# Four small moves in a convolution, scan and attention kernel: products three states ahead, gated sums sooner, x loaded first, the shortest output last

## The chip, the cores and the metric

The kernel runs on one core of a Trainium2 chip. A core has five engines that run side by side, each with a queue of its own: TensorE (PE, matrix products; PEld is its loading of weights), VectorE (DVE), ScalarE (ACT), GpSimd (POOL) and SyncE (SP, which here only issues DMAs). They meet through semaphores. Times are microseconds (us) of device time for one execution. The profile is one more execution, recorded by the hardware.

## What is computed

Input x has 8 images of 128 channels with 16 x 16 pixels, all float32. Four layers follow each other:

- an "adder" convolution: for each of 128 filters f, minus the sum over channels and 3 x 3 taps of |W - x|, on normalised images;
- a Mamba block with three scan directions, two images (512 columns) at a time:

```
uc    = silu(causal_conv1d(u))
delta = softplus(dt @ dw.T + db)
h_t   = exp(delta_t * A) * h_(t-1) + (delta_t * u_t) * B_t      # 16 states per channel
y     = sum over states of h * C + u * D
```

  and then an attention between the directions, a gate with silu(z) and two 3 x 3 convolutions;
- an attention layer with random features, and a mixture of experts;
- a spectral layer, whose result is the output.

## The kernel before

**Adder layer** (`adder_layer`, `start`). Eight images lie beside each other, 128 channels on the partitions. x is loaded as four pairs of images: pairs 0 and 2 are issued on SP's queue, pairs 1 and 3 on ACT's. Behind them on SP stand the weights w of this layer and of the next ones, and behind them on ACT three shared tables (`cst`, `vecs`, `rows`). `start` normalises the images pair by pair: a sum on DVE (L333), a mean through a product on PE (`mu`), squares on ACT (`sq`), their sums, a variance through a product (`var`), and the scaled images `sh` in three shifted copies. Between these small products PE is given spare ones (`meanwhile`), whose results nobody reads. Then PE sums the taps of x into `px`, in six taps of four blocks of two images, and the columns of w into `wsum`; in the first tap `wsum` products stand between the blocks. After that, for each filter and tap, DVE (a maximum, L450 and L446) or ACT (an absolute value, L452) makes `d`, 2048 columns, and PE sums it over the channels into `o`. `d` has four buffers for each of the two engines.

**Scans** (`_scans`). Twelve units (four pairs of images, three directions) of 16 states each make 192 states r, with n the state within its unit. For each state:

- POOL multiplies `du` (delta times u) by a row of B into `dbu` (`inputs`, L814), three buffers;
- ACT makes the decays `da` (`decays`, L827), in PSUM, three buffers;
- DVE runs two scans (L909), one for each half of the channels, and multiplies the result `st` by a row of C that ACT copied to PSUM (`pcs`, L819; L920). For n = 1 and n = 8 (`AWAY`) POOL makes that product instead (L918);
- PE adds the states up in `acc`.

The rows of B and C come back from DRAM, spread over all partitions, in chunks of two states (`bs` and `cs`, L803), two buffers each, issued on SP. While a unit is scanned, `prepare` makes the inputs of the next one step by step: on POOL these are `uc` (L688), for each half of the channels two steps of `delta` (L668, L669), and `du` (L699). Beside that `other` runs the attention and convolutions of the pair before: `images` advances two attention chains a turn at a time, and from a certain turn on the gated sums of `gated` (L1059, L1061, L1063) on POOL; `gates` puts L604 on POOL. The loop below sets the order on PE, DVE, ACT and POOL; what SP issues is ordered by the framework's scheduler, except where the program pins it. The first unit (`first_unit`) is written out by itself; it has spare products of its own.

**Spectral layer** (`spectral_layer`). Five groups of columns are accumulated in PSUM over all filters; at the end each group gets its last three taps, an addition with the residual X on DVE (L1876) and a DMA to the output (L1882). The groups go from the one with the fewest columns (256) to the largest (512).

Of the kernel before, what the change touches and what calls it, by code (L numbers as in the profile page):

```python
# [10 lines left out]
F32 = mybir.dt.float32  # L11
# [5 lines left out]
P = 128  # L17
B = 8
# [3 lines left out]
NBLK = NT // BLK  # L22
# [3 lines left out]
NST = 16  # L26
# [197 lines left out]
class Env:  # L224
# [30 lines left out]
        self.diag = early.tile([P, 3, 2, 5, P], F32, tag="diag", name="diag")  # L255

    def load_shared(self):
        nc = self.nc
        nc.scalar.dma_start(self.cst[:, P:], self.dram["cst"][:, P:])
        nc.scalar.dma_start(self.vecs, self.dram["vecs"])  # L260
        nc.scalar.dma_start(self.rows, self.dram["rows"].partition_broadcast(P))

    def load_weights(self):
        for k, t in self.w.items():
            self.nc.sync.dma_start(t, self.dram[k])
        self.nc.sync.dma_start(self.diag, self.dram["diag"])

    def c(self, name):
        a, b = self.cols["cst"][name]
# [37 lines left out]
MAX_TAPS = (0, 2, 4, 6, 8)  # L307
# [7 lines left out]
def start(E, pool, psum, x, shifted):  # L315

    nc = E.nc
    spare = psum.tile([P, P], F32, tag="px", name="spare")

    def meanwhile(n):  # L320

        for _ in range(n):
            E.mm(spare, E.ones, E.ones)

    def small(name):
        return pool.tile([P, B], F32, tag=name, name=name)

    s1, neg_mu, s2, rs = (small(n) for n in ("s1", "neg_mu", "s2", "rs"))
    sq = pool.tile([P, B, L], F32, tag="sq", name="sq0")
    pairs = [slice(2 * i, 2 * i + 2) for i in range(NBLK)]  # L330
    meanwhile(6)
    for b in pairs:
        nc.vector.tensor_reduce(s1[:, b], x[:, b, :], AX.X, ALU.add)  # L333
        mu = psum.tile([P, 2], F32, tag="st", name="mu0")
        E.mm(mu, E.c("group"), s1[:, b])
        meanwhile(2 if b is not pairs[-1] else 1)
        nc.scalar.copy(neg_mu[:, b], mu)
        for i in range(b.start, b.stop):
            nc.scalar.activation(sq[:, i, :], x[:, i, :], AF.Square, bias=neg_mu[:, i : i + 1])
    for b in pairs:  # L340
        nc.vector.tensor_reduce(s2[:, b], sq[:, b, :], AX.X, ALU.add)
        var = psum.tile([P, 2], F32, tag="st", name="var0")
        E.mm(var, E.c("group"), s2[:, b])
        meanwhile(1 if b is not pairs[-1] else 2)
        nc.scalar.activation(rs[:, b], var, AF.Sqrt, bias=E.eps, scale=-1.0)
    for b in pairs:
        nc.vector.reciprocal(rs[:, b], rs[:, b])
        for i in range(b.start, b.stop):
            dst = shifted[1][:, i, 1:17, :].rearrange("p h w -> p (h w)")
            nc.vector.tensor_scalar(dst, x[:, i, :], neg_mu[:, i : i + 1], rs[:, i : i + 1], ALU.add, ALU.mult)  # L350
        nc.scalar.copy(shifted[0][:, b, 1:17, 1:16], shifted[1][:, b, 1:17, 0:15])
    for i, b in enumerate(pairs):
        op = nc.vector.tensor_copy if i < 2 else nc.scalar.copy
        op(shifted[2][:, b, 1:17, 0:15], shifted[1][:, b, 1:17, 1:16])


def adder_layer(E):
# [8 lines left out]
    with ExitStack() as ctx:  # L366
# [10 lines left out]
        for i in range(NBLK):  # L377
            two = slice(2 * i, 2 * i + 2)
            (nc.scalar if i % 2 else nc.sync).dma_start(x[:, two, :], E.dram["x"][two].rearrange("b c s -> c b s"))
        w = p.tile([P, 9, P], F32, tag="w", name="w0")  # L380
        nc.sync.dma_start(w, E.dram["adder"])
        E.load_shared()
        E.load_weights()

# [22 lines left out]
            kh, kw = divmod(k, 3)  # L407
            return shifted[kw].rearrange("p b h w -> p b (h w)")[:, :, kh * 16 : kh * 16 + L]

        def add(out, lhsT, src, start, stop, blocks=range(NBLK)):  # L410

            for i in blocks:
                E.mm(out[i * FG : (i + 1) * FG, :], lhsT, src[:, 2 * i : 2 * i + 2, :], start, stop)

        px = ps.tile([P, BLK], F32, tag="px", name="px0")
# [1 line left out]
        with tc.manual_schedule(engines={nc.tensor.engine, nc.vector.engine, nc.scalar.engine}):  # L417
            nc.scalar.preload_act_table_set(SQRT)
            start(E, p, ps, x, shifted)

            wsum = [ps.tile([P, 1], F32, tag="st", name="wsum") for _ in range(2)]
            weights = [(pw, taps, k) for pw, taps in zip(wsum, (MAX_TAPS, MORE_TAPS)) for k in taps]
            for n, k in enumerate(PX_TAPS):
                for i in range(NBLK):
                    add(px, neg[:, int(k in MORE_TAPS), :], tap(k), n == 0, n == len(PX_TAPS) - 1, (i,))
                    for pw, taps, t in weights[2 * i : 2 * i + 2] if n == 0 else ():
                        E.mm(pw, w[:, t, :], E.ones[:, 0:1], start=t == taps[0], stop=t == taps[-1])

# [104 lines left out]
def _scans(E, ctx, F):  # L535
# [165 lines left out]
    def first_unit(k, s, p, new, pre, sig, proj):  # L701
# [66 lines left out]
        for h, (tag, scratch) in enumerate((("f", "ln_xc"), ("cs", "ln_rstd"))):  # L768
            pd = ps.tile([P, UT], F32, tag=tag, name="pd")
            E.mm(pd, w_dt[:, k, h * P : (h + 1) * P], proj[0:DTR, :])  # L770
            one_e = one.tile([P, UT], F32, tag=scratch, name="one_e")
            halves.append((pd, delta[:, h, :], pre[:, h, :], sig[:, h, :], one_e))

        for h, (pd, d, e, r, one_e) in enumerate(halves):
            db = E.v("db" + s, h)
# [34 lines left out]

    def inputs(r):
        if r < states:
            dbs[r] = three.tile([P, 2, UT], F32, tag="db", name="dbu")
            nc.gpsimd.tensor_tensor(dbs[r], got[r // NST]["du"], bc(row("bs", r), 1, 2), ALU.mult)  # L814

    def rows_of_c(r):
# [50 lines left out]
    with tc.manual_schedule(engines={nc.tensor.engine, nc.vector.engine, nc.scalar.engine, nc.gpsimd.engine}):  # L867
        new, *rest = tiles()
        got[0].update(new)
        first = first_unit(*units[0], new, *rest)  # L870
        next(first)
        for c in range(2):
            chunk("bs", 0, c)
            chunk("cs", NST, c)
        dbs[0] = three.tile([P, 2, UT], F32, tag="db", name="dbu")
        for h in range(2):
            next(first)
            nc.vector.tensor_mul(dbs[0][:, h, :], new["du"][:, h, :], row("bs", 0))
            decays(h)
            if h == 0:  # L880
                rows_of_c(0)
        inputs(1)
        next(first)
        decays(2)
    acc = late = None
    room = 0
    other = _Chain(beside())

# [3 lines left out]
    with tc.manual_schedule(engines={nc.tensor.engine, nc.vector.engine, nc.scalar.engine, nc.gpsimd.engine}):  # L892
        for r in range(states):
            i, n = divmod(r, NST)
            k, s, p = units[i]
            if r % (len(BRANCHES) * NST) == 0:
                F.y[p] = F.two.tile([P, 3, 2, UT], F32, tag="y", name="y")
            if n == NST - 2:
                while not more.done:
                    more.advance()  # L900
                more = _Chain(prepare(*units[i + 2], got[i + 2]) if i + 2 < len(units) else iter(()))
            if r % CN == 0:
                chunk("bs", 0, r // CN + 2)
            inputs(r + 2)
            st = four.tile([P, 2, UT], F32, tag="st", name="st")
            for h in range(2):
                g = 2 * r + h
                da = das[g % 3].rearrange("p b l -> p (b l)")
                nc.vector.tensor_tensor_scan(st[:, h, :], da, dbs[r][:, h, :], 0.0, ALU.mult, ALU.add)  # L909
                decays(g + 3)  # L910
            if n == 0:
                if i:
                    result(i - 1, acc)
                acc = ps.tile([P, 2, UT], F32, tag="acc", name="acc")
                for h in range(2):
                    E.mm(acc[:, h, :], E.diag[:, k, h, 4, :], got[i]["uc"][:, h, :], start=True, stop=False)
            if n in AWAY:
                nc.gpsimd.tensor_tensor(st, st, bc(row("cs", r), 1, 2), ALU.mult)  # L918
            else:
                nc.vector.tensor_tensor(st, st, bc(pcs[r][:, :], 1, 2), ALU.mult)  # L920
            rows_of_c(r + 1)
            if r % CN == 0:
                chunk("cs", NST, r // CN + 2)

            ready, late = ([], st) if n in AWAY else ([t for t in (st, late) if t is not None], None)
            for t in ready:
                for h in range(2):
                    E.mm(acc[:, h, :], ident, t[:, h, :], start=False, stop=n == NST - 1)
            room = min(room, 0) + SHARE - more.advance() - (2 if n == 0 else 0)
            if room > 0:  # L930
                room -= other.advance(room)
# [7 lines left out]
class _Fuse:  # L939
# [33 lines left out]
    def images(self, p):  # L973
# [6 lines left out]
        while not (a.done and b.done):  # L980

            a.advance()
            yield b.advance()
            if 4 <= n < 10:
                gate.advance()
            n += 1
            yield LATER
# [813 lines left out]
def spectral_layer(E, W, out):  # L1801
# [8 lines left out]
    with ExitStack() as ctx:  # L1810
# [57 lines left out]
        nc.sync.dma_start(mu, E.dram["Mu"].rearrange("i d t e -> d i t e"))  # L1868
        W.running(E, [mu[:, i].rearrange("p t e -> p (t e)") for i in range(4)])
        X = E.X.rearrange("p (b l) -> p b l", l=L)  # L1870
        for j, (i, lo, hi, b0, b1) in enumerate(groups):
            for k in range(TAPS):
                tap = u[:, b0:b1, TAPS - 1 - k + lo : TAPS - 1 - k + hi]
                E.mm(acc[j], mu[:, i, k, :], tap.rearrange("p b (i q) -> p b q i", q=2), start=False, stop=k == TAPS - 1)
# [45 lines left out]
```

## Time and profile before

| | |
|---|---|
| Runs, median (lowest to highest) | 2990.8 us (2988.36 to 2991.7, 3 runs) |
| The profiled execution's own time | 2994.82 us |
| Its span in the profile | 2993.0 us |
| PE busy | 2857.9 us (95%) |
| DVE busy | 2421.7 us (81%) |
| ACT busy | 2268.3 us (76%) |
| POOL busy | 700.4 us (23%) |
| Start to the first `o` product | 0 to about 30 us |
| Adder | to 953 us |
| Scans | 984 to about 1700 us |
| Attention layers, experts | to about 2760 us |
| Spectral layer | to 2993 us |

A row of the profile names line, engine, operation, `output<-inputs` by the program's tile names, shapes and a count; then busy time and mean, and after the second bar how long the engine stood idle just before such instructions and who ended most of that. In the timeline a row has start, length and, in brackets, the idle time before it. In the chain, each row is a stretch of the work that ended last. Busy shares are averages over stages; within a stage the wait that ends last counts. All but 24 of the 192 states cost DVE at least 3.57 us.

### The profile page before, as it was taken

The page shows a single profiled execution, that of the slowest core. Times are in us where ns is not written, and L with a number is a line of the kernel's source. Part 1 is how long each engine was busy: PE and PEld are TensorE (multiplying, and loading weights), DVE is VectorE, ACT ScalarE, POOL GpSimd, SP SyncE. Part 2 cuts the span into 40 slices and gives each one's busy share as a digit, 9 for nine tenths or more (in the row PEclk, how much of TensorE's full clock was granted, in tenths as well). Part 3 has the DMA queues.
Part 4 walks back from the last instruction along what each step waited for, and adds up shares of the span by engine and source line. Part 5 has one row for each costly group of instructions (what it writes and reads, how often), then busy time and mean ns, then how long its engine had stood idle before and what let it go on. Part 6 is the DMA issues. An engine that isn't in the chain of part 4 may idle for free.

```text
span 2993.0 us, 41823 instructions
## 1 busy us (share of the span) xinstructions
PE 2857.9 (95%) x16404; PEld 1281.7 (43%) x16404; DVE 2421.7 (81%) x3398; ACT 2268.3 (76%) x2740; POOL 700.4 (23%) x415
## 2 busy tenths in 40 slices
PE   9999999999999788998898998999999999999999
PEld 4222222222223233443343454556555555664444
DVE  7999999999998899999899747887787787885210
ACT  7999999999997777777777434477878887778332
POOL 0000000000000799998999500000000000000100
PEclk9999999999999999999999999999999999999999
DMA  1000000000000534444343200000000000001100
GB/s 68 1 1 5 1 1 5 1 1 5 1 1 5 174 145 146 135 148 144 125 163 135 101 4 25 14 1 14 14 1 14 14 12 3 14 1 45 51 28 14
DMA packets 39482, 133.46 MB, mean 45 GB/s; under 512 B 7522, under 2 KB 10732, under 8 KB 37748
## 3 DMA queue, kind: packets, MB, share of 16 engines
q1 hardware_dynamic: 38164, 129.46, 12.5%
q8 instruction: 129, 2.11, 0.3%
q10 hardware_dynamic: 1120, 1.32, 0.1%
q14 instruction: 69, 0.57, 0.1%
HBM read 127.88 MB, written 1.84 MB: 43 GB/s over the span
## 4 chain that ended last, share of the span: by engine, by line
PE 68%; DVE 15%; ACT 9%; POOL 4%; issue 3%; DMA 1%; DVEq 0%; ACTq 0%; POOLq 0%
PE o L289 29%; PE p L289 8%; DVE st L909 5%; PE acc L289 5%; PE g L289 4%; PE conv L289 3%; PE pc L289 2%; PE var L289 2%; PE pf L289 2%; POOL dbu L814 2%; PE pa L289 1%; ACT L1173 1%; PE pq L289 1%; ACT da L827 1%; PE pconv L289 1%
## 5 line engine op out<-in xcount | busy, mean ns | idle before, releaser
L289 PE MATMUL o<-d,sel 128*32 128x512 f32 x8512 | 921.5, 593 | 2.0 <-DVE d L446 1.2
L452 ACT ACTIVATE d<-sh,w 128x2048 f32<-128x2048 f32 x472 | 900.2, 1995 | 28.6 <-PE o L289 28.5
L450 DVE TENSOR_SCALAR d<-sh,w 128x2048 f32<-128x2048 f32 x592 | 718.4, 1281 | 15.0 <-PE o L289 14.9
L814 POOL TENSOR_TENSOR dbu<-du,bs 128x1024 f32<-128x1024 f32 x191 | 446.6, 2365 | 980.2 <-DVE du L786 974.7
L289 PEld LDWEIGHTS o<-d,sel 128*32 128x32 f32 x8512 | 278.3, 110 | 644.5 <-issue 533.5
L909 DVE TENSOR_TENSOR_SCAN st<-da,dbu 128x512 f32<-128x512 f32 x384 | 446.3, 1207 | 18.1 <-POOL dbu L814 14.2
L289 PE MATMUL acc<-st,cst 128*128 128x512 f32 x768 | 375.2, 621 | 52.9 <-DVE st L920 52.6
L827 ACT ACTIVATE da<-delta,neg_a 128x510 f32<-128x510 f32 x384 | 257.6, 687 | 78.6 <-DVE st L909 73.2
L289 PEld LDWEIGHTS acc<-st,cst 128*128 128x128 f32 x768 | 144.5, 196 | 252.6 <-issue 143.8
L920 DVE TENSOR_TENSOR st<-st,pcs 128x1024 f32<-128x1024 f32 x168 | 205.2, 1222 | 18.8 <-ACT pcs L819 1.5
L446 DVE SCALAR_TENSOR_TENSOR d<-sh,w,d 128x2048 f32<-128x2048 f32 x88 | 206.8, 2350 | 1.9
L1855 ACT COPY ug<-p 128x512 f32<-128x512 f32 x128 | 75.1, 587 | 132.1 <-PE p L289 132.1
L1173 ACT ACT_TABLE_LOAD x130 | 166.8, 1283 | 2.3
L1396 POOL TENSOR_TENSOR lw<-lw,turn 128x640 f32<-128x640 f32 x8 | 10.1, 1256 | 668.7 <-DVE turn L1395 579.1
L819 ACT COPY pcs<-cs 128x512 f32<-128x512 f32 x168 | 98.0, 583 | 53.6 <-DVE st L920 48.3
L289 PE MATMUL conv<-pad,f 128*128 128x512 f32 x288 | 135.0, 596 | 0.9 <-ACT pad L1071 0.6
L289 PE MATMUL p<-un,lw 128*128 128x512 f32 x256 | 121.9, 598 | 0.3 <-ACT g L1181 0.3
L289 PE MATMUL p<-g,lw 128*128 128x512 f32 x256 | 116.4, 597 | 3.2 <-ACT g L1181 3.1
L289 PE MATMUL g<-ug,me 128*128 128x512 f32 (+1 forms) x320 | 112.0, 509 | 0.0
L289 PE MATMUL p<-T,H 128*128 128x512 f32 x256 | 111.6, 592 | 0.0
L1181 ACT ACTIVATE ex<-ex 128x352 f32<-128x352 f32 x128 | 62.2, 494 | 59.1 <-DVE ex L1664 57.8
L289 PE MATMUL pf<-lw,rk 128*128 128x352 f32 x256 | 95.5, 468 | 2.9 <-DVE ek L1614 1.3
(366 smaller groups left out, 3918.6 us busy)
## 6 DMA issues: line engine op xcount, KB each, us to landing
bs<-rows SPq DMA_DIRECT2D x96, 512.0 KB, 3.7
cs<-rows SPq DMA_DIRECT2D x96, 512.0 KB, 4.6
m<-in_Mphi SPq DMA_DIRECT2D x8, 1024.0 KB, 4.9
lw<-in_layers SPq DMA_DIRECT2D x8, 948.0 KB, 4.7
f<-in_fuse SPq DMA_DIRECT2D x2, 1152.0 KB, 9.9
T<-in_T SPq DMA_DIRECT2D x1, 2064.0 KB, 7.7
diag<-in_diag SPq DMA_DIRECT2D x1, 1920.0 KB, 7.2
total<-sums SPq DMA_DIRECT2D x16, 64.0 KB, 2.0
```

The costliest lines, as they stand in the source:

```text
L289: self.nc.tensor.matmul(out, lhsT=lhsT, rhs=rhs, start=start, stop=stop)
L446: nc.vector.scalar_tensor_tensor(d, tap(k), wk, d, ALU.max, ALU.add)
L450: nc.vector.tensor_scalar(d, tap(k), wk, None, ALU.max)
L452: nc.scalar.activation(d, tap(k), AF.Abs, scale=-1.0, bias=wk)
L814: nc.gpsimd.tensor_tensor(dbs[r], got[r // NST]["du"], bc(row("bs", r), 1, 2), ALU.mult)
L819: nc.scalar.copy(pcs[r], row("cs", r))
L827: nc.scalar.activation(das[g % 3][:, :, 1:], d[:, :, 1:], AF.Exp, scale=a)
L909: nc.vector.tensor_tensor_scan(st[:, h, :], da, dbs[r][:, h, :], 0.0, ALU.mult, ALU.add)
L920: nc.vector.tensor_tensor(st, st, bc(pcs[r][:, :], 1, 2), ALU.mult)
L1173: S.tc.keep_in_program_order(S.nc.scalar.preload_act_table_set(name))
L1181: S.nc.scalar.activation(out, src, func, **kw)
L1855: nc.scalar.copy(dst, p4)
```

## The change

Five edits:

- **Loads.** The shared tables and weights are issued on SP, pinned in order, behind a tiny DMA into a new tile `there` that reads one column of images 5 and 7 of x, so that it waits for the last two pairs. ACT's queue keeps a first piece of `cst` and its two pairs of x.
- **Start of PE's work.** All `wsum` products stand ahead of `px`; the two spare products after the last variance are left out. The first scan unit gets 19 spare products after the two products `pd`; the two `acc` products that stood around `pd` now follow them.
- **Products with B.** `dbu` has four buffers; at state r POOL is given the product r + 3, but at the end of a unit (where r + 3 belongs to the next one) only r + 2.
- **Gated sums.** They begin at turn 2 of `images` instead of 4.
- **Last outputs.** The groups are closed in the reverse order, the largest first.

On DVE, ACT and PE the order of the scans' instructions is as before; on POOL single products change place, and on SP the chunks of B and C strictly alternate.

```diff
     def load_shared(self):
-        nc = self.nc
-        nc.scalar.dma_start(self.cst[:, P:], self.dram["cst"][:, P:])
-        nc.scalar.dma_start(self.vecs, self.dram["vecs"])
-        nc.scalar.dma_start(self.rows, self.dram["rows"].partition_broadcast(P))
+        self.load(self.cst[:, P:], self.dram["cst"][:, P:])
+        self.load(self.vecs, self.dram["vecs"])
+        self.load(self.rows, self.dram["rows"].partition_broadcast(P))
 
     def load_weights(self):
         for k, t in self.w.items():
-            self.nc.sync.dma_start(t, self.dram[k])
-        self.nc.sync.dma_start(self.diag, self.dram["diag"])
+            self.load(t, self.dram[k])
+        self.load(self.diag, self.dram["diag"])
+
+    def load(self, dst, src):
+        self.tc.keep_in_program_order(self.nc.sync.dma_start(dst, src))
...
-        meanwhile(1 if b is not pairs[-1] else 2)
+        meanwhile(1 if b is not pairs[-1] else 0)
...
+        there = p.tile([P, 2], F32, tag="there", name="there")
+        tc.keep_in_program_order(nc.sync.dma_start(there, x[:, B - 3 : B : 2, 0]))
         w = p.tile([P, 9, P], F32, tag="w", name="w0")
-        nc.sync.dma_start(w, E.dram["adder"])
+        tc.keep_in_program_order(nc.sync.dma_start(w, E.dram["adder"]))
...
-            weights = [(pw, taps, k) for pw, taps in zip(wsum, (MAX_TAPS, MORE_TAPS)) for k in taps]
+            for pw, taps in zip(wsum, (MAX_TAPS, MORE_TAPS)):
+                for k in taps:
+                    E.mm(pw, w[:, k, :], E.ones[:, 0:1], start=k == taps[0], stop=k == taps[-1])
             for n, k in enumerate(PX_TAPS):
-                for i in range(NBLK):
-                    add(px, neg[:, int(k in MORE_TAPS), :], tap(k), n == 0, n == len(PX_TAPS) - 1, (i,))
-                    for pw, taps, t in weights[2 * i : 2 * i + 2] if n == 0 else ():
-                        E.mm(pw, w[:, t, :], E.ones[:, 0:1], start=t == taps[0], stop=t == taps[-1])
+                add(px, neg[:, int(k in MORE_TAPS), :], tap(k), n == 0, n == len(PX_TAPS) - 1)
...
             halves.append((pd, delta[:, h, :], pre[:, h, :], sig[:, h, :], one_e))
+        meanwhile(19)
...
-            dbs[r] = three.tile([P, 2, UT], F32, tag="db", name="dbu")
+            dbs[r] = four.tile([P, 2, UT], F32, tag="db", name="dbu")
...
+    made = 1
...
-            inputs(r + 2)
+
+            while made < r + 3 and (made < r + 2 or (made + 1) // NST == i):
+                made += 1
+                inputs(made)
...
-            if 4 <= n < 10:
+            if 2 <= n < 8:
                 gate.advance()
...
-        for j, (i, lo, hi, b0, b1) in enumerate(groups):
+
+        for j, (i, lo, hi, b0, b1) in reversed(list(enumerate(groups))):
```

More of the change, by code (lines that the diff above doesn't have):

```diff
@@ L408, in tap, with add @@
             return shifted[kw].rearrange("p b h w -> p b (h w)")[:, :, kh * 16 : kh * 16 + L]
-        def add(out, lhsT, src, start, stop, blocks=range(NBLK)):
-            for i in blocks:
+        def add(out, lhsT, src, start, stop):
+            for i in range(NBLK):
                 E.mm(out[i * FG : (i + 1) * FG, :], lhsT, src[:, 2 * i : 2 * i + 2, :], start, stop)
@@ L874, in _scans @@
             chunk("cs", NST, c)
-        dbs[0] = three.tile([P, 2, UT], F32, tag="db", name="dbu")
+        dbs[0] = four.tile([P, 2, UT], F32, tag="db", name="dbu")
         for h in range(2):
```

## The prediction

> **What bounds the kernel now.** I read the chain that ended last first, then the busy time by stage, then the waits inside the stages that the change touches.
>
> ```profile
> PE 68%; DVE 15%; ACT 9%; POOL 4%; issue 3%; DMA 1%; DVEq 0%; ACTq 0%; POOLq 0%
> 30.00:955.00 925.00, 922.78 (x8528) 279.90 (x8520) 912.20 (x681) 894.84 (x477) 0.00 (x0) 1.00 0.01 2
> 985.00:1700.00 715.00, 633.19 (x1507) 270.71 (x1508) 667.03 (x603) 533.34 (x878) 638.32 (x308) 0.97 0.42 145
> ```
>
> The second and third lines are stages (start:end, length, then PE, PEld, DVE, ACT, POOL busy). From 30 to 955 us (the adder) PE is busy 922.8 of 925: what comes before 30 us is a pure start-up delay. From 985 to 1700 us (the scans) DVE leads with 667 of 715, and POOL has 638: each holds the other up at places. The rest of the span is untouched but for the last few us.
>
> ```profile
> 9.25 0.69 DVE L333 TENSOR_REDUCE s<-x 128x2 f32<-128x512 f32 x1 [2.67 <-DMA x<-in_x]
> ...
> 15.04 1.92 PE L289 MATMUL px<-sh,neg 128*32 128x512 f32 x2
> 16.89 1.01 PE L289 MATMUL wsum<-ones,w 128*128 128x1 f32 x4
> ...
> 23.41 6.24 PE L289 MATMUL px<-sh,neg 128*32 128x512 f32 x41
> ```
>
> Start-up (start, length). The last pair of images lands at 9.25. Then px and wsum alternate until 23.41 at 1.92 and 1.01 us a turn; from 23.41 px alone runs 41 passes in 6.2 us.
>
> ```profile
> L909 DVE TENSOR_TENSOR_SCAN st<-da,dbu 128x512 f32<-128x512 f32 x384 | 446.3, 1207 | 18.1 <-POOL dbu L814 14.2
> ...
> 1035.63 1.27 POOL L668 TENSOR_TENSOR sig<-sig,pre 128x512 f32<-128x512 f32 x1 [2.84 <-ACT sig L667]
> ...
> 1039.42 2.36 POOL L814 TENSOR_TENSOR dbu<-du,bs 128x1024 f32<-128x1024 f32 x1
> 1041.73 2.35 POOL L699 TENSOR_TENSOR du<-delta,uc 128x1024 f32<-128x1024 f32 x1
> 1044.17 2.35 POOL L814 TENSOR_TENSOR dbu<-du,bs 128x1024 f32<-128x1024 f32 x1
> ...
> 1057.04 4.44 DMA cs<-rows
> 1061.56 0.60 ACT pcs L819
> ```
>
> The scans wait 14.2 us for products (dbu), 13 times. POOL sits idle 2.84 us for ScalarE with the next product queued behind (state 15), and two scans then wait for it. The last two lines are of the chain: a row of C lands 4.44 us after the POOL product L918 that frees its buffer, and its copy goes straight into the next multiplication.
>
> [...] px passes cost 0.21 us at 23.41 and 0.107 from 26.48. [...] x's last pair, issued at 1.7, took 7.6 us beside w and cst, the first 3.3. [...]
>
> **1. Loads of x first; wsum ahead of px; spare products.** ACT's queue loses three DMA issues that hold its table load until 5.66; the first mean is copied at 6.95 though PE had it at 5.34: copied now at about 5.4. The last pair of x (1 MB in all at the 370 GB/s of that stretch, from 2.3 on) lands near 6 instead of 9.25. What then limits is PE's row of mean and spare products: mu by 1.28 each from 4.76, the fourth at 8.5 instead of 10.08: **-1.58**. The variances follow at 0.85 as before, DVE and ACT ahead of them. Two spare products after the last variance go: **-1.06**. Then wsum runs unbroken, 3 x 0.94 = 2.82, and px dense, 48 passes: six more than the 42 that took 23.48 to 30.07, at 0.213 while cold. So from the last variance to the first o: before 15.11 to 30.07 = 14.96; after 2.82 + 1.28 + 6.59 = 10.69: **-4.27**. Sum **-6.9**. [...] DVE and ACT must feed PE that much sooner: at the old start of o they stood idle 9.83 and 7.66 us with full buffers and they start 1.2 us sooner, which covers 6.9. If that cover were gone, DVE's 912 of 925 would become the limit.
>
> Added: the marker DMA on SP waits for images 4 to 7 (about 6.2), and behind it on SP stand w, cst, vecs, rows and all weights. w issues at about 6.8; with 3.3 us to landing as the first x had it is there at 10.1, with the 7.1 it took in company at 13.9. It is needed at 12.5: 0 to +1.4; I take 0. cst, rows and diag are needed after 35 us.
>
> **2. 19 spare products in the first scan unit.** 38 passes at 0.12 (17 took 2.06) = 4.6 us on an idle PE, which stood 9.35 us and came back cold (the first pconv 6.12 us, the second 3.58). They move acc (1.12) from before pd to after: pd starts at 973.9 instead of 974.77, on the path: **-0.85**. PE's gap shrinks from 9.35 to some 4 us; cold time falls, pconv ends 1 to 2.5 us sooner, and the 1.35 us that a scan waits at 994.62 for the decay behind it on ACT goes: between 0 and -1.35, I take **-1**.
>
> **3. Products three ahead in four buffers.** Product r+3 reuses the buffer of r-1, as r+2 did with three, so nothing new is awaited; at a unit's end the loop stops at two ahead. In the new order on POOL only single products change place: product 7 goes ahead of uc (L688), 12 and 15 ahead of the two L668. They fill idle gaps (about 3 us before most L688, 0.4 to 5 before the second L668), POOL is 2.36 us further on at each, and du follows its delta directly. All 13 waits could go: -14.2. Some come back elsewhere: the product that frees the C buffer (L918, second state of a unit) now stands behind one more dbu. From the end of delta (1038.24) to its end there are as many instructions as before, so it still ends at 1057.02, the C row lands at 1061.5 and the multiplication of state 20 starts at 1062.2 as now. The 2.4 us gained at states 15 and 16 are lost there. The same reading gives, in unit 8, 0.9 lost; in unit 4, 0.5 of 3.7 (its L918 ends 2.5 sooner, two gated sums being out of the way); in unit 11, where a gated sum comes in between, 0.8 of 2.8. In the other units the row has 1 us to spare. Sum -14.2 + 4.6 = **-9.6**; bounds -14.2 and 0.
>
> Its SP side: a B row for products 4, 5 is asked for when product 1 is done, and is now wanted two products (4.7 us) later, not three and L918; landing has a median of 3.9 us: no wait. At a unit's start the C row for states 2, 3 now stands behind that B row on SP, until product 1 is done (1047.7 in unit 1); it lands near 1052.5 and its copy ran at 1053.1: 0, or some 0.5 us in unit 1, which ends in the same wait at state 20.
>
> **4. Gated sums two turns sooner.** Six instructions of 1.27 us per pair on POOL, same number. They wait for transposes that ended some 9 us earlier (1179.8 against 1188.7). Counted in 3: the 3.52 us wait at 1227.72 came of two of them standing before a product. Of its own: 0.
>
> **5. Shortest output last.** PE's total is the same; the last addition is 0.42 instead of 0.69, the last DMA has the same 2.3 us to landing: **-0.27**. [...]
>
> Sum: -6.9 - 0.85 - 1 - 9.6 - 0.27 = **-18.6** on the profiled execution (2994.8, span 2993.0): 2976.2. The shown runs have a median 4.0 below it: **2972**.
>
> **Rivals.** *A: the products' gain does not reach the end*, because C rows, ACT's decays or PE's attention steps (DVE waits 8.4 us for pa) take the waits over. For: PE is busy 99.6 of 100 us from 1500 to 1600. Against: PE itself idles 2 to 4 us for DVE after most of the long waits. Then only 9.0 remains: 2982. *B: more than forecast*: [...] unit boundaries lose nothing: -24, 2967. *C, slower: B rows late.* The row for products 4, 5 decides when L918 runs, that when the C row lands. If B rows land 4.7 + 1 us or more after issue (the longest seen is 7.9), every further us costs one in each of 11 units; at 8 us, 25 us against 9.0 gained elsewhere: 3007. Equal to before is 6.5 us. For: B and C rows now stand back to back on SP. Against: the B row is first of the two, and 3.9 is typical. *D: no change*: products gain nothing and w comes late: 2986 to 2989.
>
> **How the numbers follow.** Forecast 0.57 (own range 2966 to 2979), A 0.20, B 0.10, D 0.07, C 0.06. 0.2% of 2990.8, about what a measurement of this kernel can tell from no change, is 6 us: faster means below 2984.8: 0.57 + 0.20 + 0.10 = 0.87; same 0.07; slower 0.06. The range leaves out D, C and the end of B: 2963 to 2985.
>
> **What would show it.** Right: x's last reduce near 6.6, the first o near 23, the adder's end near 946; no wait for dbu over 0.7 us; a wait of some 2 us for pcs in unit 1. Wrong: wsum waiting for w; L909 still waiting for dbu; DVE waiting for pcs in most units; long landings of bs.

## The result, and the profile after

| | before | after |
|---|---|---|
| Runs, median (lowest to highest) | 2990.8 us (2987.88 to 2992.47, 5 runs) | 2976.12 us (2974.12 to 2976.46, 5 runs) |
| The profiled execution's own time | 2994.82 us | 2974.14 us |
| Its span | 2993.0 us | 2972.4 us |
| First `o` product | 29.06 us | 20.88 us |
| Start of the first scan | 984.07 us | 973.26 us |
| First scan to the end of the last | 714.39 us | 706.83 us |
| From there to the end | 1294.6 us | 1292.3 us |

The ratio is 0.9946, with a 95% interval of 0.9934 to 0.9959: the change makes the kernel 16 us faster, within 4 us. The forecast was 2972, range 2963 to 2985. The two profiled executions differ by 20.7, more than the medians (14.7); the experiments below show part of the reason.

The chain that ended last, and the same two stages in busy time (start:end, length, then PE, PEld, DVE, ACT, POOL), of the kernel after:

```profile
PE 73%; DVE 14%; ACT 8%; issue 2%; POOL 2%; DMA 1%; DVEq 0%; ACTq 0%; SPq 0%; POOLq 0%
21.00:946.00 925.00, 922.88 (x8534) 283.34 (x8523) 912.09 (x681) 895.62 (x478) 0.00 (x0) 1.00 0.01 2
974.00:1681.00 707.00, 632.17 (x1502) 271.40 (x1502) 666.26 (x601) 531.29 (x878) 638.04 (x308) 0.96 0.43 146
```

The adder is the same block of 925 us, only nine sooner. The scans hold the same work (DVE 666, PE 632, POOL 638) in 707 us instead of 715. POOL's share of the chain fell from 4% to 2%, PE's rose from 68% to 73%.

The start-up in the timeline (start, length):

```profile
4.96 1.87 DVE L335 TENSOR_REDUCE s<-x 128x2 f32<-128x512 f32 x3 [0.43 <-DMA x<-in_x]
...
10.99 2.23 PE L291 MATMUL wsum<-ones,w 128*128 128x1 f32 x12 [0.58 <-DMA w<-in_adder]
13.15 8.02 PE L291 MATMUL px<-sh,neg 128*32 128x512 f32 x48
20.88 13.59 PE L291 MATMUL o<-d,sel 128*32 128x512 f32 x124
```

The last sums of x start at 6.2, not 9.25. `wsum` is one block, and waits 0.58 us for w, which the marker now holds back; `px` is one block behind it.

What DVE waited for in the scans, before and then after (waiting group, releaser, total, times, longest). The 14.2 us for `dbu` of before stood in the prediction.

```profile
DVE mx L1018 <- PE pa L289: 8.4, 4, 4.3
DVE st L909 <- ACT da L827: 3.5, 5, 1.4
DVE st L920 <- ACT pcs L819: 1.5, 3, 0.8
DVE xn L582 <- ACT var L579: 1.3, 1, 1.3
```

```profile
DVE mx L1027 <- PE pa L291: 8.6, 5, 4.3
DVE st L918 <- ACT da L832: 7.0, 13, 1.3
DVE xn L586 <- ACT var L583: 2.5, 1, 2.5
DVE st L929 <- ACT pcs L824: 2.5, 3, 1.0
DVE st L918 <- POOL dbu L819: 1.2, 2, 0.6
```

The products' wait is all but gone: 14.2 to 1.2, none over 0.6. But 13.0 us of waits removed shortened the scans by only 7.56. ScalarE's decays took up 3.5 of it and the C rows' copies 1.0. Another 1.2 stand at a norm step (`xn`), and these are the clock's, not the change's:

```profile
1070.52 6.63 PE L291 MATMUL acc<-st,cst 128*128 128x512 f32 x8 [2.96 <-DVE st L929]
```

These eight passes of PE, behind which the norm's product stands, took 6.63 us here, 5.40 before, and 3.70 in a second trace of the changed kernel. In all 14 traces the wait for the norm goes with the granted TensorE clock around them: none where it was full (8 traces), 1.31 where it was at half for one step of 3.4 us (3), 2.55 to 2.60 where for 6.8 us (3).

Where the C row is late, in unit 1, the chain of waits shows it:

```profile
1043.74 2.37 POOL dbu L819
1046.11 2.33 POOL st L927
...
1048.46 3.57 DMA cs<-rows
...
1052.10 0.60 ACT pcs L824
...
1052.72 0.04 DVE st L929
```

POOL's product of the unit's state 1 (L927) now stands behind one more `dbu`. It frees the C buffer, the next row lands 3.57 us later, and its copy goes straight into DVE's multiplication of state 20, which waited 0.88 us. Another 0.96 fell at state 18: 1.84 in unit 1, where the forecast had 2.4, all at state 20. The rest, 0.66, is at state 4 of the first unit.

### The profile page after: what moved, and what is told of

Read it like the earlier page. It is cut to its first block, busy times and chain, and to the rows that moved or that the text cites. A ratio compares the mean times of both kernels' runs of the same rounds, so it can differ in the third digit from the quotient of the medians.

```text
span 2972.4 us, 41903 instructions
## 1 busy us (share of the span) xinstructions
PE 2850.0 (96%) x16438; PEld 1283.8 (43%) x16438; DVE 2420.7 (81%) x3398; ACT 2264.0 (76%) x2740; POOL 699.7 (24%) x415
## 3 DMA queue, kind: packets, MB, share of 16 engines
HBM read 127.88 MB, written 1.84 MB: 44 GB/s over the span
## 4 chain that ended last, share of the span: by engine, by line
PE 73%; DVE 14%; ACT 8%; issue 2%; POOL 2%; DMA 1%; DVEq 0%; ACTq 0%; SPq 0%; POOLq 0%
PE o L291 30%; PE p L291 8%; PE acc L291 7%; DVE st L918 4%; PE conv L291 4%; PE g L291 4%; PE var L291 2%; PE pconv L291 2%; PE pf L291 2%; PE pc L291 2%; PE pa L291 1%; ACT L1182 1%; PE pq L291 1%; PE po L291 1%; PE pn L291 1%
## 5 line engine op out<-in xcount | busy, mean ns | idle before, releaser
L929 DVE TENSOR_TENSOR st<-st,pcs 128x1024 f32<-128x1024 f32 x168 | 205.1, 1221 | 19.8 <-ACT pcs L824 2.5
```

## The experiments

Three stages are compared over all traces: from the start to the first scan, the scans, and the rest. A figure "of the trace" is from one profiled execution; ratios are over many runs, against the kernel before in the same session.

### Start-up: the loads alone, wsum alone, both

`load` is the first edit alone (tables and weights on SP behind the marker), `wsum` the second (`wsum` ahead of `px`, no spare products after the last variance), each on the kernel before; the third has both.

```diff
+        there = p.tile([P, 2], F32, tag="there", name="there")
+        tc.keep_in_program_order(nc.sync.dma_start(there, x[:, B - 3 : B : 2, 0]))
...
-        meanwhile(1 if b is not pairs[-1] else 2)
+        meanwhile(1 if b is not pairs[-1] else 0)
...
+            for pw, taps in zip(wsum, (MAX_TAPS, MORE_TAPS)):
+                for k in taps:
+                    E.mm(pw, w[:, k, :], E.ones[:, 0:1], start=k == taps[0], stop=k == taps[-1])
```

> The kernel before with the loads alone changed (x first behind a marker, all shared loads on SP). Forecast's reading: only PE's row of mean and variance products moves, by 1.6 us; wsum and px still alternate: 2989.2 us, first o near 28.4 in the profile. Rival (the loads are what the start hung on, the place of wsum adds little): 2985 or less, first o near 25. Second rival (w, now behind x, makes wsum wait): 2991 or more.

> The kernel before with wsum ahead of px and without the two spare products after the last variance. Forecast's reading: -1.1 for the spare products and -4.3 for px in one dense row: 2985.5 us, first o near 24.7. Rival (the loads matter, this little): 2989.5. [...]

> Both of the parts above together, nothing else of the change. Forecast's reading: they add up, -6.9: 2983.9 us; the profile of the whole change, whose adder ended 9 us sooner, says 2982. Rival (DVE and ACT can't feed PE that much sooner, so the gain is lost within the adder): 2988 or more, with PE waiting for d.

Measured: the loads alone 0.9991 (0.9981 to 1.0001), wsum alone 0.9980 (0.9970 to 0.9990), both 0.9971 (0.9959 to 0.9982): -2.7, -6.0 and -8.7 us of 2991. The parts add up. The interval of the loads alone reaches from zero to -5.7, so it does not settle which of its expectations held. In the trace of `wsum` alone, with the loads as before, the last pair of x had come by 7.94, and `wsum` began at 12.60, only 0.23 later than with both. In five traces with the old loads DVE's last sum of x began between 7.94 and 9.49; the 9.25 of before is one of the late ones. The start of the kernel with both:

```profile
12.37 2.70 PE L291 MATMUL wsum<-ones,w 128*128 128x1 f32 x12
15.00 8.18 PE L291 MATMUL px<-sh,neg 128*32 128x512 f32 x48
23.00 11.33 PE L291 MATMUL o<-d,sel 128*32 128x512 f32 x104
```

This is the forecast's step 1 line by line: the last variance done at 12.5 (forecast 12.47), `wsum` 2.70 (2.82), `px` some 8 (7.87), the first `o` at 23.0 (23.2). But a single trace of the start says less than it seems to. The loads alone, expected at 28.4, had the first `o` at 20.66, with full clock from 8.7; and the next kernel, whose start is that of before, had it at 24.81, with the same instructions that took before to 29.06:

```profile
15.28 1.71 PE L289 MATMUL px<-sh,neg 128*32 128x512 f32 x2
16.93 0.61 PE L289 MATMUL wsum<-ones,w 128*128 128x1 f32 x4
17.46 1.05 PE L289 MATMUL px<-sh,neg 128*32 128x512 f32 x2
18.44 0.61 PE L289 MATMUL wsum<-ones,w 128*128 128x1 f32 x4
```

A turn of `px` and `wsum` takes 1.5 us here, 2.8 in the profile of before. The trace's record of the granted TensorE clock says why. Full clock was first granted at 26.1 us in before and 25.8 in the kernel with the gated sums alone, but at 16.7 and 15.9 in two others with the old order. With `wsum` in one block ahead of `px` it was 18.3 to 20.8 in all seven traces (in the changed kernel's it had been full from 4.7 to 11.5 and fell back). The steps of the record are multiples of 3.41 us, at a phase that differs between executions: 26.12 in before and 4.67 in the changed kernel, both starts of full clock, lie 6.28 steps apart. The phase alone does not decide it: 15.9 and 26.1 lie three steps apart, so the steps fell alike in both, but `px` began at 14.15 in the one and at 15.04 in the other. So in four traces the old start has two lengths, some 5 us apart, and the profile of before shows the long one.

### The products with B alone

```diff
-            dbs[r] = three.tile([P, 2, UT], F32, tag="db", name="dbu")
+            dbs[r] = four.tile([P, 2, UT], F32, tag="db", name="dbu")
...
-            inputs(r + 2)
+            while made < r + 3 and (made < r + 2 or (made + 1) // NST == i):
+                made += 1
+                inputs(made)
```

> The kernel before with the products three ahead in four buffers alone, gated sums where they were. Forecast's reading: as in the sum (-9.6), less 2 at state 64, where two gated sums still stand before a product: -7.5, 2983.3 us; waits for dbu fall from 14.2 to about 3 us, waits for pcs rise by 1 to 3. Rival A (waits only change their name, to pcs, da and mx): within 2 us of the kernel before, 2989 or more. Rival C (B rows late): slower than before.

Measured: 2980.95 us, 0.9975 (0.9966 to 0.9984), -7.5 us: the expectation's size. Of the 3.4 us of waits for `dbu` left, 2.17 is one, at state 64:

```profile
1220.46 2.34 DVE L913 TENSOR_TENSOR_SCAN st<-da,dbu 128x512 f32<-128x512 f32 x2 [2.17 <-POOL dbu L814]
```

The scans took 706.54 us, as in the whole change. The waits moved as there: decays 6.7, C rows 2.1, and the norm's 2.5 with the same 6.8 us of half clock.

### The products taken out of the whole change

The diff above, reversed.

> The whole change with the products with B put back: two states ahead, three buffers. Theory: the products are worth the same inside the change as alone (7.5 us), less what the earlier gated sums keep of the 3.52 us wait at state 64: +5 to +7.5 on the changed kernel, so about 2982.5 beside 2976, and waits of DVE for dbu back at 10 to 11 us in sum. Rival: in the whole change the C row, the decays and the attention steps take most of the gain, and putting the products back costs +2 at most.

Measured: 2977.7 us, 0.9959 (0.9945 to 0.9973); the scans 708.33, with 10.9 us of waits for `dbu` and none for C rows. Against the whole change (0.9946 above, 0.9938 below) the ratios make the products worth 4 to 6 us, but the intervals overlap. The rival's +2 is not excluded.

### The gated sums taken out, and alone

```diff
-            if 2 <= n < 8:
+            if 4 <= n < 10:
                 gate.advance()
```

That is the diff of the first; alone, the same lines are reversed.

> The whole change with the gated sums back at turn 4. The products alone on the kernel before gave as much in the scans (7.85 us of the trace) as the whole change did (7.56 us), so the theory is that the earlier gated sums add nothing to the products: 0 on the changed kernel (-1 to +1), though the scan of state 64 waits some 2.2 us for its product again. Rival: the 3.52 us wait needed both edits, and this costs +2 to +3.

> The gated sums two turns sooner alone, on the kernel before. The scans of the five kernels with products two ahead and sums at turn 4 took 709.0 to 714.4 us of the trace (mean 712.1), the one with products two ahead and sums at turn 2 took 708.3, the three with products three ahead 706.5 to 707.4. Theory: the sums alone shorten the wait of state 64 from 3.5 to about 1.2 us, and pay 1.2 back at state 56, where the attention step then waits: scans 709 to 712, time -1 (0 to -2.5). Rival: they are worth as much as the products, 708 and -4.

Measured: taken out of the whole change 2974.99 us, 0.9944 (0.9932 to 0.9957): no loss that the intervals show. The scan of state 64 comes 1.72 us later again, and states 56 and 68 take 1.24 and 0.63 less; but state 56 differs by 1.89 between two traces of the changed kernel itself, so its part is no proof of a payback. Alone they gave 2985.86 us, 0.9983 (0.9973 to 0.9993), -5 us, with scans of 712.58, where the trace has -1.8. The trace supports the theory and the time the rival; this stays open. What they agree on is that beside the products no further gain is seen: the two edits shorten the same wait, of state 64.

### The spare products alone

```diff
             halves.append((pd, delta[:, h, :], pre[:, h, :], sig[:, h, :], one_e))
+        meanwhile(19)
```

> The 19 spare products alone, on the kernel before. Forecast on record: -1.85 (pd 0.85 sooner, 1 from a warmer TensorE). From the traces since: from the adder's last sum to the first scan the kernel before took 31.4 us, three variants without the spare products 30.4, the whole change 29.5; so the pd part should show as 0.9 and the warmth as less: -0.9 to -1.6. Rival: 38 cold passes take longer than the idle time they fill and delay pconv: 0 or slower.

Measured: 2988.84 us, 0.9994 (0.9987 to 1.0), -1.8 us (0 to -3.9).

```profile
969.67 4.51 PE L289 MATMUL spare<-cst 128*128 128x128 f32 x38
...
980.14 6.21 PE L289 MATMUL pconv<-u,diag 128*128 128x512 f32 x8 [3.92 <-ACT u L789]
```

The 38 passes take 4.51 us (forecast 4.6; 6.13 in the changed kernel, whose clock was at half there). From the adder's last product to the first scan it takes 29.6 us; with the loads or the start alone 30.5, so `pd` is worth the 0.85 forecast. (The 31.4 of before holds another 1 us of half clock: its product `var` took 2.07 us there, 1.13 here.) The 1 us of a warmer PE isn't there: the first `pconv` takes 6.21 us, as before (6.12), although PE idles 3.92 us and not 9.35, and the scan's longest wait for a decay is still 1.4.

### The product with C one state later

```diff
-AWAY = (1, 8,)
+AWAY = (2, 8,)
```

> The whole change, with GpSimd making the product with C of state 2 of each unit instead of state 1. Theory: the waits for pcs at states 18 and 20 (0.96 and 0.88 us) come of a C buffer that GpSimd's product frees late and of the C row standing behind a B row; with the product one state later in the unit, two states are left until the row that takes its buffer is needed, so both go: -1.5 to -2, pcs waits 0.7 us in sum. Rival: the next thing in line (decays on ScalarE, attention steps) takes it over: 0. Rival: the product lands between GpSimd's steps for the next unit and delays those: slower by 1 to 5.

Measured: 2993.58 us, 1.0005 (0.9996 to 1.0013): some 17 us slower than the change, all of its gain lost. The theory was right about the C row and wrong about the time. The waits for `pcs` are gone, all of them. (The direct test, a third buffer for the C rows, wasn't tried.) In their place (waits of DVE in the scans, then ACT and DVE in the timeline of unit 6, then PE there, and last PE at the same place of the changed kernel):

```profile
DVE st L918 <- ACT da L832: 27.5, 20, 2.8
```

```profile
1347.08 0.69 ACT L640 ACTIVATE pre<-pconv,vecs 128x512 f32<-128x512 f32 x1 [3.60 <-PE pconv L291]
1347.80 1.06 ACT L644 ACTIVATE sig<-pre 128x1024 f32<-128x1024 f32 x1
1348.77 1.28 ACT L832 ACTIVATE da<-delta,neg_a 128x510 f32<-128x510 f32 x2
...
1349.47 1.22 DVE L918 TENSOR_TENSOR_SCAN st<-da,dbu 128x512 f32<-128x512 f32 x1 [2.53 <-ACT da L832]
```

```profile
1341.75 1.88 PE L291 MATMUL pconv<-u,diag 128*128 128x512 f32 x4
1343.47 1.88 PE L291 MATMUL acc<-st,cst 128*128 128x512 f32 x4
1345.18 1.86 PE L291 MATMUL pconv<-u,diag 128*128 128x508 f32 x4
```

```profile
1336.47 3.58 PE L291 MATMUL pconv<-u,diag 128*128 128x512 f32 x8
```

A state whose product GpSimd makes gives PE nothing to add up in its own turn. At state 1 that lets PE run both `pconv` of the next unit without a break (8 passes, 3.58 us); at state 2 an addition of four passes stands between them. ACT waits 3.60 us for the second (2.13 in the changed kernel), and two decays, which need nothing from it, stand behind on its queue. In the scans DVE waits 20.5 us more for decays than in the first trace of the change, and they take 15.7 longer.

### wsum behind px, and buffers for the short outputs

```diff
-            for pw, taps in zip(wsum, (MAX_TAPS, MORE_TAPS)):
-                for k in taps:
-                    E.mm(pw, w[:, k, :], E.ones[:, 0:1], start=k == taps[0], stop=k == taps[-1])
             for n, k in enumerate(PX_TAPS):
                 add(px, neg[:, int(k in MORE_TAPS), :], tap(k), n == 0, n == len(PX_TAPS) - 1)
+            for pw, taps in zip(wsum, (MAX_TAPS, MORE_TAPS)):
+                for k in taps:
+                    E.mm(pw, w[:, k, :], E.ones[:, 0:1], start=k == taps[0], stop=k == taps[-1])
...
-            fin = two.tile([P, b1 - b0, hi - lo], F32, tag="fin", name="fin")
+            fin = two.tile([P, b1 - b0, hi - lo], F32, tag=f"fin{(b1 - b0) * (hi - lo)}", name="fin")
```

> The whole change with two places altered: the twelve wsum products of one column each stand behind px instead of ahead of it, and the outputs of 256 columns get buffers of their own. Theory on the first: the one-column products hold the TensorE clock down. In six kernels with wsum ahead of px it was full from 18.3 to 20.8 us on, in four with px between them from 8.7, 15.9, 16.7 and 26.1; with dense px first it should be full from about 16, and the first o stand near 21 instead of the 22.3 that the six have on average (20.88 to 23.02). Rival: the clock comes at 19 to 21 whatever stands there, and the first o is at 22.9 or later, because px waits for the scaled images. Theory on the second: the last addition waits 1.61 us for the DMA that frees its buffer; that wait goes, and from the last product to the end it takes 3.7 instead of 4.2. Time 2974 to 2976 beside 2976; slower only if the first is wrong.

The second place first. The last addition of the changed kernel, and of this one:

```profile
2968.79 0.42 DVE L1886 TENSOR_TENSOR fin<-X,g 128x256 f32<-128x256 f32 x1 [1.61 <-DMA out_y<-fin]
```

```profile
2967.07 0.42 DVE L1886 TENSOR_TENSOR fin<-X,g 128x256 f32<-128x256 f32 x1 [1.04 <-PE g L291]
```

`fin` has two buffers, so the fifth group waits for the output DMA of the third. With the long groups first that DMA, 2.6 us from issue to landing, is still under way when the last short group is summed. From PE's last product to the end of the span: 3.94 us before, 4.16 after the change, 3.58 here. With that wait gone the reversed order saves 0.36, close to the 0.27 forecast.

At the start the clock was full from 15.4 on. With `wsum` ahead it stayed full from 18.3 at the soonest, so it came sooner, as expected; that the one-column products hold it down was not measured by itself:

```profile
12.36 7.83 PE L291 MATMUL px<-sh,neg 128*32 128x512 f32 x48
20.12 1.50 PE L291 MATMUL wsum<-ones,w 128*128 128x1 f32 x12
21.55 8.79 PE L291 MATMUL o<-d,sel 128*32 128x512 f32 x80
```

The time was 2973.17 us, 0.9945 (0.9930 to 0.9960). To tell it from the change, both ran once more side by side:

> The changed kernel as it is, once more, beside v_wfin2 on the same chip. If the first profile stands for the kernel: scans of 706 to 707 us in the trace (706.83 then; variants with products three ahead lie between 703.5 and 707.4, those without between 708.3 and 714.4), the first o between 20.9 and 23.0 by when the clock becomes full, the tail 4.16 from the last product. About 2976; a ratio to before near 0.9946.

> The kernel with wsum behind px and buffers of their own for the short outputs, beside the changed kernel on the same chip. Its two places are worth 0.58 in the tail (measured) and, if the first o at 21.55 is typical against a mean of 22.3 with wsum ahead, 0.8 at the start: 1.4 faster than the changed kernel, less than the interval can tell. Rival: the 2973.2 of its first runs against 2976.1 is real, and it is 3 faster again.

Measured: the changed kernel 2972.06 us (2967.01 to 2978.16), 0.9938 (0.9926 to 0.9950); the other 2971.28 (2970.96 to 2972.36), 0.9936 (0.9923 to 0.9948). The two can't be told apart. The second trace of the other had the clock full at 17.3 and the first `o` at 22.56; the seven traces with `wsum` ahead have 22.1 on average. From the first of `wsum` and `px` to the first `o` it takes 9.2 and 10.0 us with `wsum` behind, 9.7 to 10.7 with it ahead. The changed kernel's second trace repeats its start (20.89), and shows scans of 703.48: the wait of 2.5 us for the norm was not in it.

## Why the prediction was right, and where it was not

Forecast and measurement by stage, from several traces each, since single ones differ by up to 6 us:

| | forecast | one pair of traces | means of traces |
|---|---|---|---|
| To the first scan (step 1, `pd` of 2) | -7.75 | -10.8 | -7.8: 982.2 (3, old start) to 974.4 (5, new) |
| Scans (the rest of 2; 3, 4) | -10.6 | -7.6 | -6.9: 711.6 (7, products two ahead: 708.3 to 714.4) to 704.8 (6, three ahead: 700.9 to 707.4) |
| Tail (5) | -0.27 | +0.2 | +0.2: 3.87 to 3.94 before, 4.15 or 4.16 after |

The six are the change twice, the change without its gated sums, the products alone, and twice the kernel with `wsum` behind `px`, whose scans are those of the change; the product with C one state later (722.5) is left out. The rest after the scans took 1292.0 to 1294.6 us in the traces with the old tail and 1292.3 to 1294.1 in those of the changed one but for the slower variant, so the 2.3 by which the first pair differ there is scatter. The stage means give -14.5. The two measurements of the change give -16 (12 to 20) and -18.5 (15 to 22) by their ratios, -14.7 and -19.8 by their medians. The forecast of -18.6 lies inside both intervals.

- **Step 1** held in size (-6.9; start alone by its ratio -8.7, 5 to 12), and in each piece where the clock was late in both. The gain of the loads by themselves (1.58) is not kept apart from zero. The forecast read the clock of the start from one trace; the same old start had its first `o` anywhere from 23.8 to 29.1. w came 0.58 late, inside the 0 to 1.4 given, though the forecast also lists a wait for w as a sign of being wrong. It shows in the changed kernel, where an early full clock had brought PE to `wsum` at 11.0; with `wsum` starting at 12.3 or later PE did not wait.
- **Step 2**: the 0.85 of `pd` held. The 1 us of a warmer PE failed: that wait (1.35) is 1.44 with the spare products alone. Where it was shorter in the changed kernel (0.61), the kernel with `wsum` alone, which has no such products, shows it shorter too (0.56).
- **Step 3** had the right mechanism and the wrong size. The waits for products went (14.2 to 1.2), and unit 1 lost its gain through the C row much as written. Rival C is out: GpSimd waited for one B row in each of the six traces, 0.4 to 1.5 us, as in three of the seven, and no scan waited for a product there. Single scans of DVE were no slower with the products moved: 1191 to 1225 ns before, 1189 to 1224 after, beside 638 us of POOL in both. The term mis-sized is what re-forms, and where. Foreseen was 4.6, all through C rows. By DVE's waits, the means of the six traces against the seven, there is 1.6 more for C rows, 3.2 more for ACT's decays (3.2 to 5.0 in the seven, 6.3 to 7.8 in the six) and 1.4 for attention and norm steps, together 6.2 against 11.9 removed; of the 1.4, 0.7 is the norm's, which is the clock's. The C rows were late at states 4, 18 and 20; the 2.2 foreseen in units 4, 8 and 11 did not show beyond 0.3. Rival A named the decays and attention steps, so it was right by half. That the decays are late because DVE no longer pauses for ACT to catch up is argued, not shown.
- **Step 4**: zero on top of the products, as far as the intervals tell. Alone it is -5 (2 to 8) by the ratio, -1.8 by the trace.
- **Step 5** had the wrong sign, by 0.5 us. It counted the addition and the DMA, and not the wait of 1.61 us for the buffer that in the reversed order the DMA of the third group still holds.
- **The offset**: the whole -18.6, read from one profile, was in effect taken from the median of the runs, 4.0 below that profile. But part of what step 1 gains is that profile's late clock, which not every execution of the old kernel has. Its first scan came 1.9 us after the mean of the three, its scans took 2.8 more than the mean of the seven.

So the start met its forecast on the means, and the scans fell short by 3.7 of 10.6. That the first median still came within some 4 us of 2972 is in part luck: single traces differ by up to 6 us in one stage.

## What to carry to other kernels

Where an engine stands idle for another in front of queued work, making the stock one deeper can remove that wait (here 14.2 to 1.2 us), but ask which engine is late next before you count all of it as time; here ScalarE's decays and the C rows took most of the half that was lost. Before you reverse or rotate a loop, see which buffer each step reuses and whether the transfer that holds it has landed by then; and before moving one state's work to another engine, see which instructions on the third engine close the gap that it leaves. A stage whose clock may still be at half needs more than one trace (here the old start, to its first `o`, took from 23.8 to 29.1 us).

## What was unexpected of the hardware

- The same instructions at the start took TensorE to its first `o` at 23.8, 24.8, 28.8 and 29.1 us, with full clock from 15.9, 16.7, 25.8 and 26.1. The record moves in steps of 3.41 us.
- Full clock was lost in the middle of work: in the changed kernel's trace it was granted at 4.7 and taken back from 11.5 to 18.3, while PE went from small products to twelve of one column and into `px`. The second trace of that kernel has the same times within 0.03 us (`wsum` 2.23 and 2.25, `px` 8.02 and 7.99).
- In the seven traces with `wsum` ahead of `px`, full clock (in the changed kernel, its return) came at 18.3 to 20.8, and not at a fixed time after `px` began: `px` from 15.00, full from 20.73; `px` from 14.96, full from 18.82. In the two with `wsum` behind it came at 15.4 and 17.3 (`px` from 12.4 and 12.6). What in the work decides the moment was not measured.
- The steps of TensorE's clock reach the other engines: DVE's wait for the norm step was 0, 1.31 or about 2.6 us in the 14 traces, by whether TensorE stood at half clock for no step, one or two.
